# Reordering and merging the transfers behind a staged activation in a four-direction state-space kernel

## The chip, the cores and the metric

The kernel runs on one core of a Trainium2 chip. The metric is the device time of one execution in microseconds. The kernel before was timed in 3 runs: median 1778.31 us, from 1777.98 to 1785.43.

## What is computed

The input `x` is (4, 128, 96, 96) in float32. It is group-normalised (32 groups), read as a sequence of 9216 positions in four directions (rows forward and backward, columns forward and backward), sent through the same small network in each, and the four results are fused and added to `x`:

```python
t = grouped1x1(x, in_proj_w, in_proj_b)          # 4 groups, 128 -> 512 channels
u, gate = silu(t[:, :256]), t[:, 256:]
u = depthwise_conv(u, dw_w)                      # 5 taps along the sequence
s, bb, cc = ssm_in(u), tanh(ssm_b(u)), tanh(ssm_c(u))
a = 0.999 + 0.0009 * sigmoid(ssm_delta(u))
prefix = cumsum(log(a))
hst = exp(prefix) * cumsum(bb * s * exp(-prefix))  # h = a*h + bb*s
u = u + ssm_out(cc * hst + ssm_d * s)
y = out_proj(grouped1x1(u * sigmoid(gate), mix_w, mix_b))
out = x + fuse_w @ concat(y of the 4 directions) + fuse_b
```

All arithmetic is float32.

## The kernel before

**Tiling.** There are 8 phases, one for each batch and each axis (V, then H; phase 0 is batch 0's V). A phase walks its sequence from both ends at once, in 6 steps of 1536 positions; a step is split by the position's residue modulo 4 into 4 residues of 384 columns. One **iteration** (`pair_on(t)`, 24 to a phase, 192 in all; the first six are `pair(t)`) does one residue for the forward and the backward direction. Steps 12 to 17 are phase 2, iteration 48 is its first.

**Fresh and mirrored steps.** The first 3 steps of a phase are fresh: `x` is projected and its silu computed, for both ends. In the last 3 the two directions have swapped places, so the silus and gates of the first 3 serve again: those of steps 3 and 4 are still in SBUF, step 5's were written to DRAM during step 0 (`keep_silu`) and come back by `load_silu`; gates are all written to DRAM (`kept`) and read back by `load_kept`, 768 KB each, two iterations ahead.

**The front.** An iteration t prepares residue g of a step five iterations ahead (the *front* `ahead = t + 5`; a step's four fronts end two iterations before its first iteration). `new_front` gives four matmuls from `x_in` (two tiles, one for each end, four residues each); `new_silu` writes the second half of the channels straight into the step's `sil` tile; `new_stage` (L506-533) writes the first half into a staging tile (`shared` in the profile, L517), because the conv wants it with channels and residues exchanged, and four DMAs of 96 KB carry it over to `sil` (L525, `sil<-shared`). Behind them `new_stage` issues three loads of the next step's `x_in` (L297: 64, 32 and 32 partitions, since the last group of channels of the backward end uses residue g where the others use 3-g), and in step 0 the stores of the second half (L559, `sil<-sil`) and of the stage (L561, `front<-shared`); in other steps an `edge` store (L533). In step 0 the first column is zeroed by GpSimd (L521, L523) before those DMAs.

**Order.** The program is written out by hand, each engine runs its instructions in that order, and nearly all DMAs are issued by SyncE (SP). An iteration's DMAs stand in this order: loads of `lone`, reload of `acc` and store of `out` (L1050, L902: at the start of an H-to-V phase the finished batch leaves and the next comes in), statistics chunks `xs` of the next batch (L429, read by VectorE's `bn_stats` L437), gate loads, `load_kept` (L675), and the front's DMAs. Each of SP's DMAs signals one of eight semaphores, DMAHW0 to DMAHW7, in turn, and waits until the last DMA on the same one has landed: the ninth waits for the first, whatever its data. For example the chunk that iteration 51 reads:

```order
L429 DMA xs_3_5002<-in_xr 128x384 [waits DMAHW1_49,DVE_49]
```

Iteration t on TensorE is: `conv` (L130, `sil,band`, into banks 6 and 7, which the last stage must have left), the last pair's output products (`u,w_fin`), the front's matmuls (L490) between those of the state output (L638), and the projection (`u,main`), whose tanh on ScalarE is `tm` (L845). The first `conv` of a step needs all four quarters of `sil`. For residues 1 and 2 `conv_less` adds 16 short matmuls (`sil,less`).

**The opening.** Steps 0 and 1 are built from smaller projections (`compute_front`, `front_parts`); `whole_front` does a whole front of step 2 in each of `pair(4)` and `pair(5)`, and a second one at the end of `pair(5)`.

Of the kernel before, what the change touches and what calls it, by code (L numbers as in the profile page):

```python
# [68 lines left out]
def conv_preact_kernel(  # L69
# [55 lines left out]
    def bank(i):  # L125
        return psum[:, i, :]
# [160 lines left out]
    def half(s):  # L287
        return slice(64 * s, 64 * s + 64)
# [5 lines left out]
    def load_front(step, s, r, q):  # L294
        if fresh(step):
            un = units[step * UB + s]
            nc.sync.dma_start(  # L297
                x_in[s][r, q, :], xs[un["b"], un["lay"], r, q, bass.ds(un["st"] * N, N + 1)]
            )
# [146 lines left out]
    def sil_tile(of):  # L446
        return wk.tile([P, 2, 4, 2, N + 1], F32, tag="sil", name=f"sil_{of}")

    kept_sil = [dp.tile([R, P, 2, N + 1], F32, tag=f"sil{e}", name=f"sil{e}") for e in range(2)]
# [6 lines left out]
    def front_parts(i, banks, half=False):  # L456

        step, g = divmod(i, R)
        if g == 0:
            sils[step] = new_sil(step)  # L460
        yield from compute_front(step, g, banks, half)
        if g == R - 1:
            keep_lone(step)
        after_front(step, g)

    def mirrored(i):

        step, g = divmod(i, R)
        if step * UB >= NU or fresh(step):
            return  # L470
        st = step % NS
        if st in (NS // 2, NS // 2 + 1):
            sils[step] = sils[step - 1 - 2 * (st - NS // 2)]
        elif g < 3:
            load_silu(step, (g + 1,))
        if st == NS - 2:
            for s in range(2):
                load_front(step + 2, s, half(s), slice(g, g + 1))

    def new_front(i, banks):  # L480

        step, g = divmod(i, R)
        if g == 0:
            sils[step] = new_sil(step)
        st, r = step % NS, (0, 32, 64, 96)

        def one(s, j):
            q = R - 1 - g if s > j else g
            a = slice(64 * s + 32 * j, 64 * s + 32 * j + 32)
            nc.tensor.matmul(  # L490
                bank(banks[2 * j + s])[:, : N + 1], stats[units[step * UB]["b"]][0][a, s, :], x_in[s][a, q, :],
                start=True, stop=True,
            )

        return one

    def new_silu(i, banks):

        step, g = divmod(i, R)
        bn = stats[units[step * UB]["b"]][1]  # L500
        for s in range(2):
            nc.scalar.activation(  # L502
                sils[step][:, s, 1, g, :], bank(banks[2 + s])[:, : N + 1], AF.Silu, bias=bn[:, 1:2]
            )

    stages = []  # L506
# [1 line left out]
    def new_stage(i, banks):  # L508

        step, g = divmod(i, R)  # L510
        st, bn, sil = step % NS, stats[units[step * UB]["b"]][1], sils[step]
        if g == 0 and (st == 0 or step == 2):
            sh = shared()
            stages[:] = [sh[:, e * 2 * (N + 1) : (e + 1) * 2 * (N + 1)].rearrange("p (s n) -> p s n", s=2)
                         for e in range(2)]
        stage = stages[g % 2]
        nc.scalar.activation(  # L517
            stage, psum[:, banks[0] : banks[0] + 2, : N + 1], AF.Silu, bias=bn[:, 0:1]
        )
        if st == 0:  # L520
            nc.gpsimd.memset(stage[:, g // 2, 0:1], 0.0)  # L521
            if g < 2:
                nc.gpsimd.memset(sil[:, :, 1, g, 0:1], 0.0)  # L523
        for m in range(4):
            nc.sync.dma_start(sil[32 * g : 32 * g + 32, :, 0, m, :], stage[32 * m : 32 * m + 32, :, :])  # L525
        if st < NS // 2 - 1:
            load_front(step + 1, 0, slice(0, 64), slice(g, g + 1))
            load_front(step + 1, 1, slice(64, 96), slice(R - 1 - g, R - g))
            load_front(step + 1, 1, slice(96, P), slice(g, g + 1))
        if st == 0:  # L530
            keep_silu(step, g)
        elif g in (0, R - 1):
            nc.sync.dma_start(edge_of(step)[g // 3], stage)  # L533

    def whole_front(i, banks):
        one = new_front(i, banks)
        for s, j in ((0, 1), (0, 0), (1, 0), (1, 1)):
            one(s, j)
        new_silu(i, banks)
        new_stage(i, banks)  # L540

    def edges(step, g, j, engine):
        sil = sils[step]
# [13 lines left out]
    def keep_silu(step, g):  # L557
        e = step // NS % 2
        nc.sync.dma_start(kept_sil[e][g], sils[step][:, :, 1, g, :])  # L559
        if step:  # L560
            nc.sync.dma_start(kept_front[e][g], stages[g % 2])  # L561
        else:
            nc.sync.dma_start(by_group(kept_front[e], g), sils[step][32 * g : 32 * g + 32, :, 0].rearrange("c s m n -> c m s n"))

    def by_group(t, g):
        return t[g].rearrange("(m c) s n -> c m s n", m=4)

    def load_silu(step, gs):
        if 0 in gs:
            sils[step] = new_sil(step)  # L570
        for g in gs:
            e = step // NS % 2
            nc.sync.dma_start(sils[step][:, :, 1, g, :], kept_sil[e][g])
            nc.sync.dma_start(sils[step][32 * g : 32 * g + 32, :, 0].rearrange("c s m n -> c m s n"), by_group(kept_front[e], g))

    def in_proj(step, g, s, j, bk):
        for c in range(4):
# [84 lines left out]
    def keep(n):  # L662
        return kept[n // NP % 2][n % NP]
# [313 lines left out]
    def pair(t):  # L977
        i = 2 * t
        banks = head_banks(t)
        if t == R:  # L980
            load_lone(1)
        if t:
            new_u(i)
            taps(i, range(1, K))
            single = alone(units[i]["p"])
            conv(i, banks, single)
            if single:
                add_lone(i, banks)
# [23 lines left out]
        for g in {0: (0, 1), 1: (2, 3)}.get(t, ()):  # L1012
            keep_silu(0, g)
        if t > 3:
            nc.sync.dma_start(keep(t - 4), tile_of(t - 4))
        if t > 0:
            s = tbs[i - 2][0:64, :]
            nc.gpsimd.tensor_scalar(s, s, d_sb[0:64, 0:1], None, ALU.mult)

    def pair_on(t):  # L1020
# [106 lines left out]
        if gated is not None:  # L1127
            if gated % NP > 1:
                nc.sync.dma_start(keep(gated), to)
            else:  # L1130
                nc.sync.dma_start(keep(gated)[:, :, 0], both)
        load_kept(n + 2)
        if ahead is not None:
            new_stage(ahead, spots)
        if last:
            for s in range(2):
                under(bi + 2, s)
# [8 lines left out]
        if t >= end - 4:  # L1146
            load_last(t)
        if step % NS == NS - 2 and g == R - 1:
            load_silu(step + 1, (0,))
        if n % (NP * 2) == 0:  # L1150
            send()

# [288 lines left out]
```

## Time and profile before

| what | us |
|---|---|
| median of 3 runs | 1778.31 |
| the profiled execution | 1789.02 |
| its span, first to last instruction | 1787.2 |
| TensorE matmuls busy | 1724.5 (96%) |
| VectorE, ScalarE, GpSimd busy | 1515.0, 1478.2, 1459.8 |
| DMA queue of SP | 383.06 MB, 71.0% of the 16 engines' time |

A row of the timeline gives the start, the time from the first start to the last end, engine, line, operation, tiles written and read, shape, the count of instructions merged, and in brackets the idle time of the engine just before, with what ended it. TensorE's ends are modelled, so its busy share says little; its idle times in brackets say where the program stood still. For SP a row's length is the issuing alone. PEclk is the share of the clock that TensorE was granted.

### The profile page before, as it was taken

What the parts mean: (1) busy time and instruction counts of PE and PEld (TensorE: products, weight loads), DVE (VectorE), ACT (ScalarE), POOL (GpSimd) and SP (SyncE); (2) the same over time, 40 slices, a digit from 0 to 9 for tenths busy, and PEclk for the clock granted to TensorE, in tenths of its full rate; (3) what the DMA queues carried; (4) which work ended last, traced back from release to release, by engine and by line L of the source; (5) the groups of instructions that cost most, each with busy time, mean ns of one, the idle gap of its engine ahead of it and who ended that gap; (6) DMA issues with size and microseconds to landing.
All of it is one profiled execution on the core that took longest, in us unless ns stands there. A gap on an engine that the chain in (4) does not pass through costs nothing.

```text
span 1787.2 us, 50638 instructions
## 1 busy us (share of the span) xinstructions
PE 1724.5 (96%) x20410; PEld 707.6 (40%) x20410; DVE 1515.0 (85%) x1508; ACT 1478.2 (83%) x2410; POOL 1459.8 (82%) x1466
## 2 busy tenths in 40 slices
PE   7999999999889999999989999999998999999998
PEld 3243344344343334434434343344343443344333
DVE  5799989888688998888868998888876888888897
ACT  4788888888778888888878888888887888888875
POOL 3489988988669988988867998888876899888887
PEclk9999999999999999999999999999999999999999
DMA  7755996369895798537999489843899738973375
GB/s 215 224 169 181 298 247 177 138 212 262 248 280 207 225 272 226 169 122 248 251 257 315 149 258 265 230 136 131 263 263 272 227 130 271 235 205 126 129 236 177
DMA packets 156232, 386.33 MB, mean 216 GB/s; under 512 B 22624, under 2 KB 89056, under 8 KB 156000
## 3 DMA queue, kind: packets, MB, share of 16 engines
q1 hardware_dynamic: 155856, 383.06, 71.0%
q8 instruction: 162, 2.65, 0.6%
q14 instruction: 70, 0.57, 0.1%
q10 hardware_dynamic: 144, 0.04, 0.0%
HBM read 215.12 MB, written 133.01 MB: 195 GB/s over the span
## 4 chain that ended last, share of the span: by engine, by line
PE 81%; DMA 10%; ACT 2%; DVE 2%; POOL 2%; issue 1%; SPq 1%; ACTq 0%; DVEq 0%; POOLq 0%
PE psum L130 66%; PE psum L638 6%; PE psum L618 5%; PE psum L490 4%; DMA gate<-kept 4%; DMA x_in<-in_xs 2%; DMA sil<-shared 2%; DMA kept<-shared 1%; DVE psum L808 1%; DMA front<-shared 1%; DVE u L699 1%; POOL acc L943 1%; ACT shared L517 1%; ACT psum L806 1%; DMA sil<-sil 1%
## 5 line engine op out<-in xcount | busy, mean ns | idle before, releaser
L808 DVE SCALAR_TENSOR_TENSOR psum<-sil,small,psum 128x768 f32<-128x768 f32 x576 | 589.1, 1023 | 51.9 <-ACT psum L806 33.3
L130 PE MATMUL psum<-u,w_fin 128*32 128x384 f32 (+1 forms) x6192 | 559.2, 486 | 1.1 <-ACT ys L924 0.5
L130 PE MATMUL psum<-u,main 128*32 128x384 f32 x6144 | 536.1, 490 | 0.6 <-DVE u L755 0.4
L699 DVE SCALAR_TENSOR_TENSOR u<-gate,psum 128x768 f32<-128x768 f32 x376 | 341.6, 950 | 156.9 <-PE psum L638 73.3
L943 POOL TENSOR_TENSOR acc<-ys,acc 128x384 f32<-128x384 f32 x375 | 433.8, 1178 | 19.6 <-ACT ys L924 7.3
L130 PE MATMUL psum<-sil,band 128*32 128x384 f32 x3072 | 300.3, 497 | 40.8 <-DMA sil<-shared 12.9
L130 PEld LDWEIGHTS psum<-u,w_fin 128*32 128x32 f32 x6192 | 204.9, 110 | 312.0 <-issue 212.1
L889 POOL TENSOR_TENSOR t<-t,t 64x384 f32<-64x384 f32 (+1 forms) x192 | 268.9, 1400 | 68.6 <-DVE t L883 36.0
L650 ACT COPY psum<-u 128x768 f32<-128x768 f32 x384 | 306.3, 798 | 7.2 <-DVE u L699 4.4
L130 PEld LDWEIGHTS psum<-u,main 128*32 128x32 f32 x6144 | 180.2, 110 | 327.1 <-issue 206.9
L856 POOL TENSOR_SCALAR t<-tm 64x384 f32<-64x384 f32 x188 | 177.6, 945 | 142.1 <-ACT tm L845 123.2
L638 PE MATMUL psum<-t,main 32*128 32x384 f32 x1536 | 273.1, 519 | 3.0 <-ACT psum L650 2.3
L890 POOL TENSOR_TENSOR t<-t,t 64x384 f32<-64x384 f32 (+1 forms) x192 | 235.0, 1224 | 15.1
L857 POOL TENSOR_TENSOR t<-t,tm 64x384 f32<-64x384 f32 x192 | 220.0, 1146 | 25.1 <-ACT t L848 10.0
L808 DVE SCALAR_TENSOR_TENSOR u<-sil,small,psum 128x768 f32<-128x768 f32 x192 | 194.9, 1015 | 6.8
L806 ACT ACTIVATE psum<-sil,small 128x768 f32<-128x768 f32 x191 | 171.7, 899 | 32.9 <-DVE u L699 31.5
L926 ACT COPY ys<-psum 128x384 f32<-128x384 f32 x288 | 137.9, 479 | 60.0 <-PE psum L130 51.0
L130 PEld LDWEIGHTS psum<-sil,band 128*32 128x32 f32 x3072 | 108.4, 110 | 197.2 <-issue 82.5
L618 PE MATMUL psum<-x_in,wn 32*128 32x384 f32 x768 | 162.2, 497 | 0.0
L490 PE MATMUL psum<-x_in,wn 32*128 32x385 f32 x704 | 150.1, 503 | 1.5 <-DMA x_in<-in_xs 1.4
L502 ACT ACTIVATE sil<-psum,bnorm 128x385 f32<-128x385 f32 x176 | 102.3, 582 | 54.8 <-PE psum L490 39.4
L654 ACT ACTIVATE gate<-psum,bnorm 128x384 f32<-128x384 f32 x168 | 97.2, 581 | 43.8 <-PE psum L618 27.0
(110 smaller groups left out, 1708.5 us busy)
## 6 DMA issues: line engine op xcount, KB each, us to landing
gate<-kept SPq DMA_DIRECT2D x106, 768.0 KB, 7.4
kept<-gate SPq DMA_DIRECT2D x82, 768.0 KB, 3.9
sil<-shared SPq DMA_DIRECT2D x352, 96.2 KB, 5.9
x_in<-in_xs SPq DMA_DIRECT2D x306, 96.2 KB, 3.8
sil<-sil SPq DMA_DIRECT2D x64, 385.0 KB, 5.9
lone<-edge SPq DMA_DIRECT2D x26, 770.0 KB, 8.5
out<-acc SPq DMA_DIRECT2D x46, 384.0 KB, 5.6
acc<-in_xr SPq DMA_DIRECT2D x39, 384.0 KB, 5.2
```

Of the source, the lines that this page charges most:

```text
L130: nc.tensor.matmul(o[r, : rhs.shape[-1]], lhsT, rhs, start=start, stop=stop, skip_group_check=True)
L490: nc.tensor.matmul(bank(banks[2 * j + s])[:, : N + 1], stats[units[step * UB]["b"]][0][a, s, :], x_in[s][a, q, :], start=True, stop=True,)
L618: nc.tensor.matmul(bank(to)[:, :N], stats[un["b"]][0][r, s, :], x_in[s][r, q, off : off + N], start=True, stop=True)
L638: nc.tensor.matmul(bank(ssm(bi, s) + j)[:, :N], w_so[r, bass.ts(j, P)], z[r, :], start=(bi, s) not in seeded, stop=True, skip_group_check= ...
L650: nc.scalar.copy(psum[:, ssm(bi, s) : ssm(bi, s) + 2, :N], us[bi][:, s])
L699: nc.vector.scalar_tensor_tensor(v, g, 1.0, pz, ALU.add, ALU.mult)
L806: nc.scalar.activation(part, src, AF.Copy, scale=w_tap[:, 0:1])
L808: nc.vector.scalar_tensor_tensor(us[i][:, :, 1, :] if k == K - 1 else part, src, w_tap[:, k : k + 1], part, ALU.mult, ALU.add,)
L857: nc.gpsimd.tensor_mul(ta[0:64, p, :], tb[0:64, :], tm[0:64, :])
L889: engine.tensor_mul(ta[0:64, p, r], tb[64:P, r], ta[64:P, p, r])
L890: engine.tensor_add(tb[0:64, r], ta[0:64, p, r], tb[0:64, r])
L943: adder.tensor_add(part, y, part)
```

## The change

1. In `pair_on`, `new_stage` with its four `sil<-shared` DMAs now comes ahead of `load_kept`; what followed those DMAs is split off into `new_rest`, behind `load_kept`.
2. The backward end's last group uses residue 3-g like the others, so `x_in` is loaded two residues at a time (`load_planes`), one DMA for each end, after every second front: 4 DMAs for a step in place of 12. The first step of the next phase is loaded in iterations 9 and 10 of a phase (4 DMAs) where it was 8 DMAs in iterations 12 to 15.
3. The second half of step 0's silus is stored and reloaded two residues at a time (770 KB in place of 385), and the store moves from step 0's four fronts to the first two fronts of step 1 (iterations 23 and 0 of the phase).
4. The stage's zero column is written by ScalarE right behind the stage; GpSimd's remaining memset is one for each front.
5. In the opening the second front of `pair(5)` moves into `pair_on(6)`, between its `conv` and its output products, in banks 4 and 5 used twice; `after_front`'s loads of `x_in` come ahead of `keep_lone`'s four stores.

SP's DMAs fall from 1405 to 1233 (`x_in` 436 to 296, step 0's stores and reloads 64 to 32); ScalarE gets 28 instructions more; TensorE's and VectorE's counts stay. The core of the diff:

```diff
-        load_kept(n + 2)
         if ahead is not None:
             new_stage(ahead, spots)
+        load_kept(n + 2)
+        if ahead is not None:
+            new_rest(ahead)
+        if t % NP in (9, 10) and un["step"] // NS < 2 * B - 1:
+            load_planes((un["step"] // NS + 1) * NS, t % NP - 9)
...
+    def load_planes(step, h):
+        for s in range(2):
+            load_front(step, s, half(s), bass.ts(1 - h if s else h, 2))
...
         def one(s, j):
-            q = R - 1 - g if s > j else g
+            q = R - 1 - g if s else g
...
         if st == 0:
-            nc.gpsimd.memset(stage[:, g // 2, 0:1], 0.0)
-            if g < 2:
-                nc.gpsimd.memset(sil[:, :, 1, g, 0:1], 0.0)
+            nc.scalar.activation(stage[:, g // 2, 0:1], mid, AF.Copy, scale=0.0)
+            nc.gpsimd.memset(sil[:, g // 2, 1, min(g, R - 1 - g), 0:1], 0.0)
         for m in range(4):
             nc.sync.dma_start(sil[32 * g : 32 * g + 32, :, 0, m, :], stage[32 * m : 32 * m + 32, :, :])
-        if st < NS // 2 - 1:
-            load_front(step + 1, 0, slice(0, 64), slice(g, g + 1))
-            load_front(step + 1, 1, slice(64, 96), slice(R - 1 - g, R - g))
-            load_front(step + 1, 1, slice(96, P), slice(g, g + 1))
+
+    def new_rest(i):
+        step, g = divmod(i, R)
+        st, stage = step % NS, stages[g % 2]
+        if st < NS // 2 - 1 and g % 2:
+            load_planes(step + 1, g // 2)
         if st == 0:
-            keep_silu(step, g)
+            nc.sync.dma_start(kept_front[step // NS % 2][g], stage)
         elif g in (0, R - 1):
             nc.sync.dma_start(edge_of(step)[g // 3], stage)
+        if st == 1 and step > 1 and g < 2:
+            keep_silu(step - 1, g)
...
-        if t == LAG - 1:
-            whole_front(t + R + 1, (6, 7, 2, 3))
...
+        if n == 0:
+            i0, to = t + R, (4, 5, 4, 5)
+            one = new_front(i0, to)
+            one(0, 1)
+            one(1, 1)
+            new_silu(i0, to)
+            one(0, 0)
+            one(1, 0)
+            new_stage(i0, to)
+            new_rest(i0)
         add_next(w[0])
```

How the order of instructions changes, at three places. First SP in iterations 45 and 46, where the last two quarters of step 12 are staged (`sil_4335` and `sil_4305` are step 12's tile before and after, `gate` the tiles of the kept gates). Before:

```order
L675 DMA gate_177<-kept_4_194 128x1536
L525 DMA sil_4335<-shared 32x770 x4
L297 DMA x_in_70<-in_xs 64x385
L297 DMA x_in_71<-in_xs 32x385 x2
L559 DMA sil_202<-sil_4335 128x770
L561 DMA front_204<-shared 128x770
L675 DMA gate_176<-kept_7_197 128x1536
L525 DMA sil_4335<-shared 32x770 x4
L297 DMA x_in_70<-in_xs 64x385
L297 DMA x_in_71<-in_xs 32x385 x2
L559 DMA sil_202<-sil_4335 128x770
L561 DMA front_204<-shared 128x770
```

The same two iterations after:

```order
L525 DMA sil_4305<-shared 32x770 x4
L686 DMA gate_177<-kept_4_194 128x1536
L534 DMA front_204<-shared 128x770
L525 DMA sil_4305<-shared 32x770 x4
L686 DMA gate_176<-kept_7_197 128x1536
L297 DMA x_in_70<-in_xs 64x2x385
L297 DMA x_in_71<-in_xs 64x2x385
L534 DMA front_204<-shared 128x770
```

The quarter's four DMAs stand ahead of the gate's, and 20 DMAs have become 14.

Second SP in iterations 49 to 51, with the statistics chunk `xs_3` that VectorE reads in iteration 51 and the last quarter of step 13 (`sil_4730`, `sil_4690`), of iteration 50. Before:

```order
L1050 DMA acc<-in_xr 128x2x384 x2
L902 DMA out<-acc 128x2x384 x2
L675 DMA gate_177<-kept_0_190 128x1536
L525 DMA sil_4730<-shared 32x770 x4
L297 DMA x_in_70<-in_xs 64x385
L297 DMA x_in_71<-in_xs 32x385 x2
L429 DMA xs_3_5002<-in_xr 128x384
L675 DMA gate_176<-kept_3_193 128x1536
L525 DMA sil_4730<-shared 32x770 x4
```

After, from the end of iteration 48 on:

```order
L297 DMA x_in_70<-in_xs 64x2x385
L297 DMA x_in_71<-in_xs 64x2x385
L565 DMA sil_202<-sil_4305 128x1540
L1059 DMA acc<-in_xr 128x2x384 x2
L913 DMA out<-acc 128x2x384 x2
L525 DMA sil_4690<-shared 32x770 x4
L686 DMA gate_177<-kept_0_190 128x1536
L429 DMA xs_3_4957<-in_xr 128x384
L525 DMA sil_4690<-shared 32x770 x4
```

The three loads of `x_in` just ahead of the chunk are gone; farther ahead the doubled store of the silus (`sil_202`, 770 KB) and the doubled `x_in` loads of iteration 48 have come in.

Third TensorE in the opening, from the end of `pair(5)`'s projection (`u_1_2_0`) to the first state outputs (L638, L649). Before:

```order
L130 MATMUL psum<-u_1_2_0_788,main 32x384 x16
L490 MATMUL psum<-x_in_70,wn_265 128x385 x2
L490 MATMUL psum<-x_in_71,wn_265 128x385 x2
L130 MATMUL psum<-sil_443,band 32x384 x8
L490 MATMUL psum<-x_in_70,wn_265 128x385
L638 MATMUL psum<-t_0_0_1_0_442,main 128x384 x3
```

After:

```order
L130 MATMUL psum<-u_1_2_0_786,main 32x384 x16
L130 MATMUL psum<-sil_443,band 32x384 x8
L491 MATMUL psum<-x_in_70,wn_265 128x385
L491 MATMUL psum<-x_in_71,wn_265 128x385
L491 MATMUL psum<-x_in_70,wn_265 128x385
L491 MATMUL psum<-x_in_71,wn_265 128x385
L491 MATMUL psum<-x_in_70,wn_265 128x385
L649 MATMUL psum<-t_0_0_1_0_442,main 128x384 x3
```

The four matmuls of the second front now follow the `conv` and no longer precede it; their second two use the banks of the first two.

More of the change, by code (lines that the diff above doesn't have):

```diff
@@ L447, in sil_tile @@
         return wk.tile([P, 2, 4, 2, N + 1], F32, tag="sil", name=f"sil_{of}")
-    kept_sil = [dp.tile([R, P, 2, N + 1], F32, tag=f"sil{e}", name=f"sil{e}") for e in range(2)]
+    kept_sil = [dp.tile([2, P, 2, 2, N + 1], F32, tag=f"sil{e}", name=f"sil{e}") for e in range(2)]
     kept_front = [dp.tile([R, P, 2, N + 1], F32, tag=f"front{e}", name=f"front{e}") for e in range(2)]
@@ L461, in front_parts @@
         yield from compute_front(step, g, banks, half)
+        after_front(step, g)
         if g == R - 1:
             keep_lone(step)
-        after_front(step, g)
     def mirrored(i):
@@ L474, in mirrored @@
         elif g < 3:
[L475 to L478, printed above, removed]
+            load_silu(step, g + 1)
+    def load_planes(step, h):
+        for s in range(2):
+            load_front(step, s, half(s), bass.ts(1 - h if s else h, 2))
     def new_front(i, banks):
@@ L502, in new_silu @@
             nc.scalar.activation(
-                sils[step][:, s, 1, g, :], bank(banks[2 + s])[:, : N + 1], AF.Silu, bias=bn[:, 1:2]
+                sils[step][:, s, 1, R - 1 - g if s else g, :], bank(banks[2 + s])[:, : N + 1], AF.Silu, bias=bn[:, 1:2]
             )
@@ L540, in whole_front @@
         new_stage(i, banks)
+        new_rest(i)
     def edges(step, g, j, engine):
@@ L1011, in pair @@
             load_gate(2 * n + s + UB)
-        for g in {0: (0, 1), 1: (2, 3)}.get(t, ()):
-            keep_silu(0, g)
+        if t < 2:
+            keep_silu(0, t)
         if t > 3:
@@ L1148, in pair_on @@
         if step % NS == NS - 2 and g == R - 1:
-            load_silu(step + 1, (0,))
+            load_silu(step + 1, 0)
         if n % (NP * 2) == 0:
```

29 lines of the change are left out of this document (16 added, 13 removed).

## The prediction

> **What bounds the kernel now.** I read the page first, then TensorE's idle times in its timeline, then who was late at each of them. The page's rows:
>
> ```profile
> span 1787.2 us, 50638 instructions
> ...
> PE 1724.5 (96%) x20410; PEld 707.6 (40%) x20410; DVE 1515.0 (85%) x1508; ACT 1478.2 (83%) x2410; POOL 1459.8 (82%) x1466
> ...
> sil<-shared SPq DMA_DIRECT2D x352, 96.2 KB, 5.9
> ```
>
> TensorE sets the pace; nothing in the change takes a matmul away. What can be won is the time in which it stands still. TensorE's timeline, the waits over 1 us behind the start-up's first, with the `conv`s of two undisturbed iterations (473.39 and 481.75) for comparison:
>
> ```profile
> 66.37 2.30 PE L490 MATMUL psum<-x_in,wn 32*128 32x385 f32 x6 [1.41 <-DMA x_in<-in_xs]
> ...
> 81.16 2.79 PE L130 MATMUL psum<-sil,band 128*32 128x384 f32 x16 [2.20 <-ACT shared L517]
> ...
> 238.61 1.67 PE L130 MATMUL psum<-sil,band 128*32 128x384 f32 x14 [1.22 <-DMA sil<-shared]
> ...
> 453.31 3.14 PE L130 MATMUL psum<-sil,band 128*32 128x384 f32 x16 [4.06 <-DMA x_in<-in_xs]
> ...
> 473.39 1.48 PE L130 MATMUL psum<-sil,band 128*32 128x384 f32 x16
> ...
> 481.75 1.48 PE L130 MATMUL psum<-sil,band 128*32 128x384 f32 x16
> ...
> 497.16 3.26 PE L130 MATMUL psum<-sil,band 128*32 128x384 f32 x14 [6.86 <-DMA sil<-shared]
> ...
> 640.66 1.50 PE L130 MATMUL psum<-sil,band 128*32 128x384 f32 x16 [1.15 <-ACT shared L517]
> ...
> 677.05 2.02 PE L130 MATMUL psum<-sil,band 128*32 128x384 f32 x14 [1.19 <-ACT shared L517]
> ...
> 890.26 1.70 PE L130 MATMUL psum<-sil,band 128*32 128x384 f32 x15 [2.15 <-DMA x_in<-in_xs]
> ...
> 934.37 3.06 PE L130 MATMUL psum<-sil,band 128*32 128x384 f32 x14 [8.15 <-ACT t L854]
> ...
> 1113.26 2.08 PE L130 MATMUL psum<-sil,band 128*32 128x384 f32 x14 [1.17 <-ACT shared L517]
> ...
> 1327.21 3.22 PE L130 MATMUL psum<-sil,band 128*32 128x384 f32 x16 [2.81 <-DMA x_in<-in_xs]
> ...
> 1368.99 3.18 PE L130 MATMUL psum<-sil,band 128*32 128x384 f32 x14 [4.77 <-DMA sil<-shared]
> ...
> 1549.62 2.13 PE L130 MATMUL psum<-sil,band 128*32 128x384 f32 x15 [2.55 <-ACT t L854]
> ```
>
> They add up to 39.7 us, and but for the first two they lie at the seams of phases. I sort them: **A**, first `conv` of phases 2, 4, 6 (453, 890, 1327): 9.02. **B**, first of phases 1, 3, 5, 7 (238, 677, 1113, 1549): 6.13. **C**, first `conv` of the second step of phases 2, 4, 6 (497, 934, 1369): 19.78. D, at 640.66: 1.15. The opening: 3.61. A `conv` after a wait also runs slower than the 1.48 us of 481.75: 1.66, 0.22 and 1.74 more in A (3.62), 1.98 in B, 5.06 in C. So A costs 12.6 us, B 8.1, C 24.8.
>
> Why A: ScalarE's timeline has the stage of step 12's last quarter (iteration 46), SP's timeline when it was sent; the last two rows are from SP's waits and from the DMA issues between 440.7 and 492.1 us (count, size, median us to landing).
>
> ```profile
> 439.59 0.89 ACT L517 ACTIVATE shared<-psum,bnorm 128x770 f32<-128x770 f32 x1
> ...
> 441.37 0.35 SPq L559 DMA_DIRECT2D sil<-sil  x1
> ...
> 443.13 0.38 SPq L675 DMA_DIRECT2D gate<-kept  x1
> 443.85 2.45 SPq L525 DMA_DIRECT2D sil<-shared  x4
> ...
> 452.92 0.34 SPq L559 DMA_DIRECT2D sil<-sil  x1
> ...
> SPq L559 <- DMA gate<-kept: 37.7, 22, 4.1
> ...
> sil<-shared SPq DMA_DIRECT2D x19, 96.2 KB, 7.5
> ```
>
> The stage ends at 440.48. SP is then still busy with iteration 45's stores: a store of this line waits for the landing of a gate, with which it shares nothing but a semaphore, 22 times for 37.7 us in all. The four transfers leave 3.4 us late, behind 768 KB of gate, and the `conv` that could start at 449.25 (453.31 less 4.06) starts at 453.31.
>
> Why C: the same lag, grown to an iteration. VectorE's rows (statistics, and the gating that frees the gate's tile), then SP's:
>
> ```profile
> 470.21 1.82 DVE L699 SCALAR_TENSOR_TENSOR u<-gate,psum 128x768 f32<-128x768 f32 x2 [1.07 <-ACT ys L924]
> ...
> 485.78 0.55 DVE L437 BATCH_NORM_STATS2 bn<-xs 128x6 f32<-128x384 f32 x1
> 492.15 0.56 DVE L437 BATCH_NORM_STATS2 bn<-xs 128x6 f32<-128x384 f32 x1 [5.81 <-DMA xs<-in_xr]
> ...
> 673.79 0.56 DVE L437 BATCH_NORM_STATS2 bn<-xs 128x6 f32<-128x384 f32 x1 [1.80 <-DMA xs<-in_xr]
> ...
> 479.91 0.47 SPq L675 DMA_DIRECT2D gate<-kept  x1
> ...
> 484.16 1.97 SPq L297 DMA_DIRECT2D x_in<-in_xs  x3
> 489.79 0.35 SPq L429 DMA_DIRECT2D xs<-in_xr  x1
> ```
>
> The gate whose tile was free at 472.03 is asked for at 479.91. The chunk, eight DMAs behind that gate, waits for its landing: SP issues nothing from 486.13 to 489.79. VectorE then stands 5.81 us, and the quarter behind the chunk keeps TensorE 6.86 us. The row at 673.79 shows the same, smaller, behind B's two waits on ScalarE.
>
> **The change part by part, against the profiled 1789.02 us.**
>
> *Staged silus first, fewer DMAs: A.* In step 0's iterations SP now has 6 or 8 DMAs where it had 10. Eight places ahead of iteration 46's first quarter transfer stands a store of iteration 45, landed by then, so it leaves at 440.5. Four issues at 0.61 (2.45 over 4) and the page's median landing of 5.9 us give 448.8, under 449.25. With the 7.5 us of the crowded stretch, taken behind the gates, it would be 1.2 us late. Nearest is the page's median, since the gate now stands behind: A goes, -12.6 (bounds -12.6, since no more is there, and -7 with 1.2 us left at each and one restart).
>
> Here a rule of the Trainium skill can be weighed. The waits of 2.15 and 2.81 us were followed by a `conv` of 1.70 and of 3.22 us, so I count 1.74 us of slow restart with the second. The Trainium skill, "TensorE: Matmul & The Clock Gate", Part 1, has the clock halved only after an idle window of about 3.4 us; by it the 1.74 would have another cause and A would give 10.9. The trace's row decides: it counts.
>
> *B.* The same cause: at 238 the quarter itself is late, at 677 the chunk (673.79 in VectorE's rows), behind which gating and stage stand. With fewer DMAs ahead of both, of 8.1 I take 7, as for A all but a remainder (bounds 4 and 8.1).
>
> *C.* Here bytes count too. What moved between iteration 46's stage and the chunk's landing, and the rate of that stretch beside that of the densest 20 us (columns of the last two: stretch, length, busy time of each engine, PEclk, DMA share, GB/s):
>
> ```profile
> q1 hardware_dynamic: 6054, 12.64, 86.6%
> ...
> sil<-sil SPq DMA_DIRECT2D x2, 385.0 KB, 4.9
> ...
> 440.70:492.10 51.40, 45.53 (x516) 20.03 (x508) 34.82 (x36) 36.94 (x60) 34.49 (x35) 0.97 0.87 248
> 500.00:520.00 20.00, 20.00 (x241) 8.22 (x237) 14.00 (x14) 15.86 (x26) 13.90 (x14) 0.98 1.04 304
> ```
>
> After, two stores of 385 KB and a front's of the same size leave the stretch and two of 770 KB come in: +0.39 MB, 13.0 MB. At 248 GB/s that takes 52.4 us, at 304 42.8. The chunk is wanted when VectorE has done the one before it, 486.33 (485.78 and 0.55), less the 5.7 us that A's first wait and restart no longer cost: 39.9 us after 440.70. So it is late by 2.9 to 12.5 us, where it is late by 5.81. The quarter (0.39 MB more) is wanted when the projection is through, 490.30 less 5.7, 43.9 us after: late by 0.2 to 10.1, now 6.86. The middles are about today's waits, so C stays at phases 2 and 4. At phase 6 no statistics are loaded (four chunks, 0.79 MB less): the quarter is late by -2.5 to +6.9 against 4.77; I take half of its 6.5 (wait and restart) away: -3. Bounds for all of C: -24.8 and +16.
>
> *Zero column.* No activation of one column lies in a front today; the nearest row is at the start:
>
> ```profile
> 2.53 0.20 ACT L341 ACTIVATE first_table<-first_table 128x1 f32<-128x1 f32 x1
> ```
>
> 28 of them: 5.6 us if all stood on the path, below nothing if GpSimd's memset had held a transfer. The stage's transfers wait for it, TensorE does not: I take +1.
>
> *Opening.* SP's rows, the stores and then the loads that end the first wait:
>
> ```profile
> 59.00 3.43 SPq L739 DMA_DIRECT2D edge<-sil  x4
> 62.53 2.47 SPq L297 DMA_DIRECT2D x_in<-in_xs  x4
> ```
>
> The loads now leave 3.5 us sooner: -1.4. The 2.20 us at 81.16 (the second front's stage holds bank 6) go, but that front now stands behind the `conv` and must wait for its own silus between its two pairs of matmuls: 0 (bounds -2.2 and +2). `x_in` two residues at a time arrives after every second front, three iterations before use; D keeps its cause: both nothing.
>
> Sum: -12.6 - 7 - 3 + 1 - 1.4 = -23.0. The profiled execution is 10.7 us above the median. The waits with their restarts are 50.4 us of it; if the 10.7 lie wholly in them, the gain shrinks to 0.79 of that, -18.1. From 1778.31 that gives 1755.3 to 1760.2; I take 1757.
>
> **The rivals.**
>
> *C goes as well.* For it: fewer DMAs mean fewer empty stretches of SP like 486.13 to 489.79, and 13.0 MB in 39.9 us is 326 GB/s, little over the 304 that was seen for 20 us. Against it: nothing here held 326 for 40 us. Price: another 21.8, with the 0.79 at least 17: 1735 to 1740. The Trainium skill, "DMA: Bandwidth & Descriptors", Specifications, puts the limit of a core's HBM traffic at about 358 GB/s; by that this rival would hold, the trace's 304 speaks against it.
>
> *C grows.* The doubled stores now lie where C is tightest. If the rate stays at 248, the chunks of phases 2 and 4 come 6.7 us later than today, the three quarters about 3: +13 to +16 over my sum, 1770 to 1773.
>
> *Gates come late: slower.* `load_kept` now waits for ScalarE's stage and four issues, some 3.5 us more. A gate has two iterations, about 17.4 us (two of the 8.36 between the `conv`s at 473.39 and 481.75, and some). Today the one of 479.91 was asked for 7.9 us late and landed just before the chunk's issue, 9.8 us on: 17.7, hidden because VectorE stood still anyway. If SP's lag stays over 4 us, gatings of iterations 49 to 51 wait some 4 us each: three seams, three gatings, +36: 1793. For it: nothing but order has changed for the gate. Against: the lag is what the fewer DMAs take away.
>
> *No effect.* The quarter lands late for lack of rate, not of order: 1778.
>
> **How the numbers follow.** Forecast 0.54 (alone 1748 to 1767), C gone 0.18, C grown 0.17, gates late 0.06, no effect 0.05. The bounds of A and B move each case by some 6 us, so the range 1735 to 1775 leaves out half of C gone, a third of C grown and the late gates, 0.2 in all. Beyond 0.5%, about what a measurement of this kernel can tell from no change (1769.4 and 1787.2): faster 0.76 (forecast, C gone, a quarter of C grown), same 0.19, slower 0.05.
>
> **What would show it.** Right: the waits at the first `conv` of phases 1 to 7 under 0.5 us with `conv`s of 1.5 us, SP's `sil<-shared` leaving within 0.5 us of the stage; `bn_stats` of iteration 51 still waiting about 6 us and the next `conv` about 7. Wrong: A's waits still 2 us or more; C under 3 us in all three places; VectorE's gating waiting for `gate<-kept`; the chain through ScalarE longer in iterations 19 to 22.

## The result and the profile after

The changed kernel takes 1760.85 us (median of 4 runs, 1758.79 to 1763.52) against 1781.57 of the kernel before in the same comparison; the ratio is 0.9884, 95% interval 0.9853 to 0.9915. The profiled execution took 1758.79 us, 30.2 less than that of before, which was a long one of its kind. The forecast of 1757 us, with its range of 1735 to 1775, holds; one term of its sum has the wrong sign, as will be seen.

The page after:

```profile
span 1757.0 us, 50266 instructions
...
PE 1713.8 (98%) x20410; PEld 705.5 (40%) x20410; DVE 1508.5 (86%) x1508; ACT 1484.5 (84%) x2438; POOL 1470.6 (84%) x1452
...
gate<-kept SPq DMA_DIRECT2D x106, 768.0 KB, 5.7
...
sil<-shared SPq DMA_DIRECT2D x352, 96.2 KB, 3.5
```

A quarter now lands 3.5 us after its issue (median), where it was 5.9. TensorE's timeline: first `conv`s of phases 2 and 4, then all waits over 1 us behind the opening.

```profile
442.59 1.75 PE L130 MATMUL psum<-sil,band 128*32 128x384 f32 x16
...
472.38 1.57 PE L130 MATMUL psum<-sil,band 128*32 128x384 f32 x16 [2.62 <-ACT shared L518]
...
485.33 1.68 PE L130 MATMUL psum<-sil,band 128*32 128x384 f32 x15 [2.85 <-ACT shared L518]
...
872.21 1.62 PE L130 MATMUL psum<-sil,band 128*32 128x384 f32 x16
...
901.82 1.50 PE L130 MATMUL psum<-sil,band 128*32 128x384 f32 x16 [2.57 <-ACT shared L518]
...
914.89 3.19 PE L130 MATMUL psum<-sil,band 128*32 128x384 f32 x16 [4.45 <-ACT shared L518]
...
1342.91 2.06 PE L130 MATMUL psum<-sil,band 128*32 128x384 f32 x15 [2.74 <-ACT shared L518]
```

The rows without brackets had no wait: A and B are gone. C is still there, but in two pieces in phases 2 and 4, and it is ScalarE's stage that is late, not the quarter itself. ScalarE is late because VectorE was; its waits for DMAs in these stretches:

```profile
469.62 1.82 DVE L710 SCALAR_TENSOR_TENSOR u<-gate,psum 128x768 f32<-128x768 f32 x2 [3.44 <-DMA gate<-kept]
...
482.11 0.56 DVE L437 BATCH_NORM_STATS2 bn<-xs 128x6 f32<-128x384 f32 x1 [4.97 <-DMA xs<-in_xr]
...
899.05 1.82 DVE L710 SCALAR_TENSOR_TENSOR u<-gate,psum 128x768 f32<-128x768 f32 x2 [3.40 <-DMA gate<-kept]
...
911.67 0.56 DVE L437 BATCH_NORM_STATS2 bn<-xs 128x6 f32<-128x384 f32 x1 [5.10 <-DMA xs<-in_xr]
...
1340.15 1.82 DVE L710 SCALAR_TENSOR_TENSOR u<-gate,psum 128x768 f32<-128x768 f32 x2 [4.42 <-DMA gate<-kept]
```

So each C now begins with a late gate, which is the mechanism of the rival "gates come late", once in a seam and not three times, and in phases 2 and 4 goes on with a late chunk. VectorE's gating waiting for a kept gate was one of the prediction's own signs of being wrong.

**Where the time went.** For all kernels below I measure one thing: the length of an iteration, from the start of its `tm` on ScalarE to that of the next. ScalarE's timeline for iterations 48 to 51 after:

```profile
451.61 0.58 ACT L856 ACTIVATE tm<-psum,small 128x384 f32<-128x384 f32 x1
...
460.81 0.58 ACT L856 ACTIVATE tm<-psum,small 128x384 f32<-128x384 f32 x1
...
472.24 0.57 ACT L856 ACTIVATE tm<-psum,small 128x384 f32<-128x384 f32 x1
...
485.18 0.57 ACT L856 ACTIVATE tm<-psum,small 128x384 f32<-128x384 f32 x1
...
494.40 0.58 ACT L856 ACTIVATE tm<-psum,small 128x384 f32<-128x384 f32 x1
```

They last 9.20, 11.43, 12.94 and 9.22 us. As undisturbed I take 9.20, 8.42, 8.25 and 9.22 (in experiment 11, where nobody waits there, phase 6 has 9.20, 8.42, 8.36 and 9.26), so C costs 7.7 us here. The same sum over iterations 0 to 5 of phases 2, 4 and 6 I call C, that over iterations 20 to 23 of the seven seams AB (undisturbed 8.88, 8.33, 8.26, 9.31 at the end of a V phase, 9.20, 8.43, 8.33, 9.23 of an H phase; with the zero column by ScalarE iteration 22 takes 8.01, which makes the small negative sums). Slow restarts and waits inside a `conv` are in both. The medians come from four comparisons, in which the kernel before took 1780.27 to 1784.28 us; the sums are of one profiled execution each.

| kernel | timed median, us | profiled execution, us | AB | C | sum |
|---|---|---|---|---|---|
| before | 1781.57 | 1789.02 | 22.5 | 28.3 | 50.8 |
| changed | 1760.85 | 1758.79 | -1.2 | 23.2 | 22.0 |
| changed, timed again | 1757.07 | 1759.06 | -1.5 | 22.0 | 20.5 |
| order only | 1763.44 | 1764.09 | 12.1 | 16.1 | 28.2 |
| x_in in pairs only | 1763.37 | 1766.45 | 8.5 | 24.8 | 33.3 |
| changed, gate ahead | 1758.42 | 1758.97 | -1.4 | 21.1 | 19.7 |
| changed, zeros by GpSimd | 1763.76 | 1761.79 | 0.2 | 25.0 | 25.2 |
| zeros by GpSimd, old opening | 1766.01 (one run) | 1766.01 | 0.4 | 27.0 | 27.4 |
| changed, stores early | 1753.45 | 1756.78 | -1.1 | 22.1 | 21.0 |
| changed, chunks moved | 1753.45 | 1754.14 | -1.2 | 17.7 | 16.5 |
| chunks moved, gate ahead | 1751.37 | 1751.32 | -1.5 | 14.9 | 13.4 |
| chunks moved, stores early | 1747.72 | 1750.55 | -1.4 | 13.6 | 12.2 |
| no stores (work left out) | 1744.10 | 1744.22 | -1.2 | 9.3 | 8.1 |
| no stores, chunks moved | 1736.08 | 1734.82 | -1.1 | 0.5 | -0.6 |

From before to after the two sums fall by 28.8 us. The first `tm` also comes 3.1 us earlier (41.5 and 38.4 us from the start; 36.9 to 41.5 over all the runs, ahead of anything that the change touches), the first seven iterations take 2.6 less (55.2 and 52.6), and iterations 17 to 19 of the seven phases 3.8 more (3.3 and 7.1 over undisturbed). Together that is 30.7 us, for the 30.2 between the two executions.

What replaced the waits is seen in the stretch from 450 to 500 us. Its columns are length, busy time of PE, PEld, DVE, ACT, POOL, PEclk, DMA share, GB/s. Before:

```profile
450.00:500.00 50.00, 39.83 (x432) 18.60 (x436) 34.70 (x36) 33.35 (x54) 32.73 (x33) 0.91 0.87 250
```

After:

```profile
450.00:500.00 50.00, 44.53 (x512) 17.96 (x508) 38.12 (x38) 38.01 (x62) 34.28 (x34) 0.97 1.03 296
```

Before, the 16 DMA engines were idle for an eighth of this stretch, since SP stood at its semaphores. After, they are full (a full set reads a little over 1 in this view). C was a question of SP's order and of bytes; experiments 4 to 7 and 11 ask how far it is now one of bytes.

### The profile page after: what moved, and what is told of

Read it like the earlier page. It is cut to its first block, busy times and chain, and to the rows that moved or that the text cites. A ratio compares the mean times of both kernels' runs of the same rounds, so it can differ in the third digit from the quotient of the medians.

```text
span 1757.0 us, 50266 instructions
## 1 busy us (share of the span) xinstructions
PE 1713.8 (98%) x20410; PEld 705.5 (40%) x20410; DVE 1508.5 (86%) x1508; ACT 1484.5 (84%) x2438; POOL 1470.6 (84%) x1452
## 4 chain that ended last, share of the span: by engine, by line
PE 86%; DMA 5%; DVE 2%; ACT 2%; POOL 2%; issue 1%; SPq 0%; ACTq 0%; POOLq 0%; DVEq 0%
PE psum L130 70%; PE psum L649 6%; PE psum L629 5%; PE psum L491 4%; DMA gate<-kept 2%; DMA kept<-shared 1%; DMA out<-acc 1%; ACT shared L518 1%; DVE t L894 1%; DMA sil<-shared 1%; DVE u L710 1%; DVE psum L819 1%; DMA acc<-in_xr 1%; POOL t L900 0%; POOL t L868 0%
## 5 line engine op out<-in xcount | busy, mean ns | idle before, releaser
L954 POOL TENSOR_TENSOR acc<-ys,acc 128x384 f32<-128x384 f32 x375 | 442.0, 1202 | 12.5 <-ACT ys L935 1.9
L130 PE MATMUL psum<-sil,band 128*32 128x384 f32 x3072 | 290.1, 489 | 19.6 <-ACT shared L518 18.0
L649 PE MATMUL psum<-t,main 32*128 32x384 f32 x1536 | 272.8, 520 | 3.0 <-ACT psum L661 2.3
L868 POOL TENSOR_TENSOR t<-t,tm 64x384 f32<-64x384 f32 x192 | 227.0, 1182 | 25.4 <-ACT t L859 10.3
L937 ACT COPY ys<-psum 128x384 f32<-128x384 f32 x288 | 138.4, 481 | 53.1 <-PE psum L130 42.6
```

Source lines behind the costliest of these rows:

```text
L130: nc.tensor.matmul(o[r, : rhs.shape[-1]], lhsT, rhs, start=start, stop=stop, skip_group_check=True)
L649: nc.tensor.matmul(bank(ssm(bi, s) + j)[:, :N], w_so[r, bass.ts(j, P)], z[r, :], start=(bi, s) not in seeded, stop=True, skip_group_check= ...
L868: nc.gpsimd.tensor_mul(ta[0:64, p, :], tb[0:64, :], tm[0:64, :])
L954: adder.tensor_add(part, y, part)
```

## The experiments

**1. Part 1 alone.** The kernel before, with the stage's four transfers ahead of the gate (what follows them is split off as `new_rest`, as in the change; the cut shows the calls alone):

```diff
-        load_kept(n + 2)
         if ahead is not None:
             new_stage(ahead, spots)
+        load_kept(n + 2)
+        if ahead is not None:
+            new_rest(ahead)
```

> The kernel before with part 1 alone: the four transfers of a stage ahead of the kept gate, everything else (twelve loads of x_in a step, stores in step 0, GpSimd's zeros, the opening) as before. Theory 'order': in step 0 the first two quarter transfers no longer stand behind a gate, so A's waits (9.0 us and 3.6 us of slow restart) fall under 1 us each and B halves; C stays at 20 us or more: 1762 to 1768. Rival 'count': the lag of SP comes from ten DMAs in an iteration, and the third and fourth quarter transfers still wait for the landing of the gate eight places ahead; A loses less than a third and the time is 1773 to 1780.

1763.44 us, ratio 0.9869 (0.984 to 0.9899). The time is what "order" said, but the split is not: AB only halves (12.1), and C falls to 16.1, at phase 6 to 0.4. At the three seams of A 3.3 us are left of 13.2, at the four of B 8.9 of 9.3. Of the waits at first `conv`s these stand in TensorE's timeline (phases 1, 2 and 3; phase 5 has one more, of 2.12 us, and within phase 0 one of 3.01 us has come in):

```profile
236.37 1.72 PE L130 MATMUL psum<-sil,band 128*32 128x384 f32 x16 [1.26 <-ACT shared L517]
...
448.31 2.15 PE L130 MATMUL psum<-sil,band 128*32 128x384 f32 x15 [1.61 <-ACT shared L517]
...
668.80 2.67 PE L130 MATMUL psum<-sil,band 128*32 128x384 f32 x16 [2.50 <-DMA gate<-kept]
```

So the order by itself takes most of A and hardly any of B. Why C shrinks beside it stays open. It is not that time lost at AB lets the queue catch up: the seam ahead of phase 6, where C all but goes (8.3 to 0.4), lost 0.6 us here and 4.6 before.

**2. Part 1 alone undone.** The changed kernel with the gate ahead again:

```diff
+        load_kept(n + 2)
         if ahead is not None:
             new_stage(ahead, spots)
-        load_kept(n + 2)
-        if ahead is not None:
             new_rest(ahead)
```

> The changed kernel with part 1 alone undone: the kept gate ahead of the stage's four transfers again. Theory 'order': A and B come back in part, 1 to 2 us with a slow restart at each of seven seams: 1766 to 1774; gating's three waits for gate<-kept (11.3 us in the changed kernel) go. Rival 'count': after parts 2 and 3 SP has no lag left at A and B, where the last quarter lands 4 us ahead of its use, so putting 768 KB of gate (2.6 us at the 297 GB/s of the crowded stretch) in front hides; A and B stay under 0.5 us, and since the gate comes earlier C shrinks: 1752 to 1760.

1758.42 us, ratio 0.9845 (0.982 to 0.9869), no slower than the changed kernel. AB is gone as before (-1.4), C is 21.1. "Count" holds. VectorE's waits:

```profile
DVE bn L437 <- DMA xs<-in_xr: 9.1, 3, 5.3
...
DVE u L710 <- DMA gate<-kept: 3.9, 1, 3.9
```

The gate's waits fall from 11.3 us to 3.9, but quarters take their place: TensorE waits 5.58 and 5.41 us in phases 4 and 6.

```profile
912.17 3.19 PE L130 MATMUL psum<-sil,band 128*32 128x384 f32 x15 [5.58 <-DMA sil<-shared]
...
1343.22 3.23 PE L130 MATMUL psum<-sil,band 128*32 128x384 f32 x14 [5.41 <-DMA sil<-shared]
```

In this full queue the order chose who waited, and hardly how long.

**3. x_in in pairs alone.** The kernel before, six loads in a step in place of twelve, the gate ahead of the stage as it was:

```diff
-        if st < NS // 2 - 1:
-            load_front(step + 1, 0, slice(0, 64), slice(g, g + 1))
-            load_front(step + 1, 1, slice(64, 96), slice(R - 1 - g, R - g))
-            load_front(step + 1, 1, slice(96, P), slice(g, g + 1))
+        if st < NS // 2 - 1 and g % 2:
+            h = g // 2
+            load_front(step + 1, 0, slice(0, 64), bass.ts(h, 2))
+            load_front(step + 1, 1, slice(64, 96), bass.ts(1 - h, 2))
+            load_front(step + 1, 1, slice(96, P), bass.ts(h, 2))
```

> The kernel before with its x_in loads two residues at a time after every second front, three DMAs for each (six a step in place of twelve); the rest, the gate ahead of the stage among it, as before. Theory 'either will do': SP's lag goes with fewer DMAs as it goes with the order, so A and B lose half or more: 1762 to 1770, iterations 22 and 23 of the even seams under 10 us each. Rival 'order': the quarters still stand behind a gate, A and B stay: 1775 to 1783.

1763.37 us, ratio 0.99 (0.9883 to 0.9916): "either will do". No first `conv` of a phase waits over 1 us, though iteration 23 still takes 10.6 to 11.1 us at five seams, more than the 10 that I expected at the even ones. C stays at 24.8. Of A 5.1 us are left, of B 3.4. So the order alone and the count alone each bring most of the change's gain; their gains overlap at A, while B falls with the count and not with the order. In the changed kernel the order could be taken back without loss.

**4. Statistics chunks a phase later.** The changed kernel, with the four chunks that phases 2 and 4 read in iterations 2 and 3 read in the next phase, as phase 0 does:

```diff
-        places = singles * 2
-        if ph == 0:
-            places = (singles[2:] + [NP + 2, NP + 3]) * 2
+        places = (singles[2:] + [(ph + 1) * NP + 2, (ph + 1) * NP + 3]) * 2
```

> The changed kernel with the four statistics chunks that phases 2 and 4 read in their iterations 2 and 3 read in iterations 2 and 3 of phases 3 and 5 (phase 0 does so already). Theory 'bytes': the waits of C come from 0.79 MB more than the queue carries there at 297 GB/s; without the chunks phases 2 and 4 lose in their iterations 1 to 3 what phase 6, which has none, loses (5.1 us over undisturbed iterations in place of 7.9 and 10.7): 8 us less, 1750 to 1754, bn_stats waits under 1 us. Rival 'gate': the late gate alone sets C, the chunk's wait only lies beside it: within 2 us of the changed kernel, 1758 to 1762.

1753.45 us, ratio 0.982 (0.9794 to 0.9846), the time that "bytes" said, though C falls by some 5 us where it said 8. What is left of C is all gate; the waits for chunks lie elsewhere:

```profile
DVE u L708 <- DMA gate<-kept: 17.7, 4, 5.9
...
DVE bn L435 <- DMA xs<-in_xr: 1.8, 3, 1.1
```

Phase 2 gained little (7.2 us of C, 7.7 with the chunks), phase 4 most (5.4, 10.5).

**5. Stores of kept silus left out.**

```diff
-        if st == 1 and step > 1 and g < 2:
+        if st == 1 and 1 < step < 2 * NS and g < 2:
```

> The changed kernel without the two stores of kept silus (770 KB each) in phases 2 to 7; the reloads read what phases 0 and 1 stored, so step 5's second half of silus is another batch's. Theory 'bytes': 1.54 MB less at 297 GB/s is 5.2 us of queue ahead of the late gate and chunk at each seam, so of the 23.7 us that C costs now 10 to 15 go: 1745 to 1751. Rival 'gate': the stores stand behind the gate that is late and the lateness is SP's waits for semaphores, so less than 4 us go: 1757 to 1761.

1744.10 us, ratio 0.9765 (0.9741 to 0.9789). C falls from 23.2 to 9.3, a fall within the 10 to 15 us expected, and is 0.1 at phase 6.

**6. The same stores in step 0 again.**

```diff
-        if st == 1 and step > 1 and g < 2:
-            keep_silu(step - 1, g)
+        if st == 0 and g % 2:
+            for s in range(2):
+                h = s if g == 1 else 1 - s
+                nc.sync.dma_start(kept_sil[step // NS % 2][h][:, :, s, :], planes_of(step, h)[:, :, s, :])
```

> The changed kernel with the kept silus stored in step 0 again, two residues of one end at a time: two stores of 385 KB after the second front and two after the fourth (iterations 20 and 22 of a phase) in place of two of 770 KB in iterations 23 and 0. Theory 'bytes': C comes from what the saturated queue carries between iterations 23 and 2; 1.54 MB less there leaves what the kernel without these stores had, about 9 us of C and none at phase 6, and 770 KB more (2.6 us at 297 GB/s) in iterations 20 and 22 hide, since the last quarters there land 4 us ahead of their use: 1745 to 1751. Rival 'A back': stores in the fronts make the quarters late again, as in the kernel with part 1 alone, whose iterations 22 and 23 lost 11.5 us: 1754 to 1762.

1753.45 us, ratio 0.9851 (0.9835 to 0.9867). Both theories miss: AB stays away (-1.1), and C hardly moves (22.1). The time is lower than the changed kernel's by less than the two intervals tell apart. The stores fill a gap between 430 and 440 us, where the DMA share goes from 0.68 to 0.92, and still nothing is won. Stretches after:

```profile
430.00:440.00 10.00, 10.00 (x115) 4.56 (x115) 7.32 (x8) 8.73 (x15) 9.39 (x11) 1.00 0.68 217
...
460.00:470.00 10.00, 9.76 (x116) 3.92 (x108) 6.32 (x8) 6.79 (x12) 9.23 (x10) 1.00 1.04 258
```

With the stores early:

```profile
430.00:440.00 10.00, 10.00 (x116) 4.49 (x118) 7.53 (x8) 8.57 (x16) 9.39 (x11) 1.00 0.92 265
...
460.00:470.00 10.00, 8.62 (x100) 3.47 (x96) 8.33 (x10) 7.47 (x12) 8.62 (x10) 1.00 1.06 234
```

From 460 to 470 the full engines move only 234 GB/s. Why a stretch with fewer bytes to carry is slower stays open. Bytes alone do not set C, then: experiment 1 too stores in step 0, with other loads of `x_in` and other zeros, and its C at phase 6 is 0.4 us, where this kernel's is 5.1.

**7. Both.** Edits 4 and 6 together:

> The two together: stores in step 0, and the statistics chunks of iterations 2 and 3 of phases 2 and 4 read one phase later. Theory 'bytes': phases 2 and 4 then carry what phase 6 does, so C is under 1 us in all three: 1736 to 1743. Rival: C has a part that hangs on neither, 1745 or more.

1747.72 us, ratio 0.9819 (0.9805 to 0.9834): the rival's side. C keeps 13.6 us, all of it gating's wait for gates (19.7 us, 6 times). Against edit 4 alone the ratio is the same.

**8. Zeros by GpSimd and the old opening.** Two edits that lie apart, in one run:

```diff
-            nc.scalar.activation(stage[:, g // 2, 0:1], mid, AF.Copy, scale=0.0)
+            nc.gpsimd.memset(stage[:, g // 2, 0:1], 0.0)
...
+        if t == LAG - 1:
+            whole_front(t + R + 1, (6, 7, 2, 3))
...
-        if n == 0:
-            i0, to = t + R, (4, 5, 4, 5)
...
```

> The changed kernel with two edits undone that lie apart in the profile: GpSimd's memset for the stage's zero column, and the opening as it was (second front in iteration 5, edge stores ahead of x_in). From the kernels that ran, the zero column on ScalarE costs 0.26 us in iteration 19 of an even seam and nothing in the others (about 1 us in all), and the first seven iterations take 33.6 us with either opening: iteration 19 at 9.4 us in place of 9.6, the first seven within 1 us of 33.7, the time within 3 us of the changed kernel. Rival (the prediction's sum): the opening costs 1.4 us more, and ScalarE's column 0.2 in each of 28 fronts, 5.6 us less.

1766.01 us in the one run, 5.2 more than the changed kernel, where I expected 3 at most. The first seven iterations take 52.9 us (52.6 in the changed kernel), and 52.6 and 53.1 in experiments 1 and 3, which have the old opening too; the kernels with the new one spread from 52.6 to 53.9. (The 33.6 and 33.7 of the expectation are iterations 3 to 6 alone.) So the opening's part is worth nothing that shows, and the 55.2 of the profile before was that execution's own. Iteration 19 is 9.37 to 9.40 us long, as expected, where it is 9.62. But C is 27.0, and that asked for the next run.

**9. Zeros by GpSimd alone**, timed beside the changed kernel on one chip:

> The changed kernel once more, beside the other three on one chip: 1757 to 1763. The theories expect the same.

> The changed kernel with part 4's new operation alone undone: GpSimd's memset writes the stage's zero column. Theory 'GpSimd holds the transfers': the stage's four DMAs wait for GpSimd, which comes to its memset 4.5 us after the stage (126.5 us in 28 fronts in the run with zero column and opening undone); SP stands still with all that is behind, and C and the kept gates of iterations 17 and 18 cost 3 to 7 us more: 1762 to 1768. Rival 'nothing either way' (the prediction took +1 for ScalarE's column): within 2 us of the changed kernel, the 1766 of that run being its scatter.

The first edit of 8 alone. 1757.07 us (1755.8 to 1760.4) for the changed kernel and 1763.76 (1761.79 to 1769.62) with GpSimd's memset; no two runs overlap. The zero column by ScalarE is worth 6.7 us. ScalarE's stage, GpSimd's memset and SP's transfers of one front, first with GpSimd's zero:

```profile
418.35 0.89 ACT L518 ACTIVATE shared<-psum,bnorm 128x770 f32<-128x770 f32 x1
...
421.51 0.10 POOL L522 MEMSET shared<- 128x1 f32 x1
...
421.64 3.13 SPq L525 DMA_DIRECT2D sil<-shared  x4
```

The same front of the changed kernel, timed again:

```profile
418.32 0.89 ACT L518 ACTIVATE shared<-psum,bnorm 128x770 f32<-128x770 f32 x1
419.24 0.20 ACT L522 ACTIVATE shared<-mid 128x1 f32<-128x1 f32 x1
...
419.47 2.42 SPq L525 DMA_DIRECT2D sil<-shared  x4
```

The memset takes 0.1 us, but GpSimd comes to it 2.3 us after the stage, and SP stands for it with the gate and all else behind. With GpSimd's zero the lengths of two iterations of phase 1 grow by 3.7 us together, AB by 1.7 and C by 3.0, and iterations 17 to 19 shrink by 3.3. In SP's waits the row for this is 124.6 us in 28 fronts here. In the kernel before it stands too, smaller since SP came late itself; GpSimd reaches its memset as late there (up to 2.7 us after the stage, here up to 2.8):

```profile
SPq L525 <- POOL sil L523: 29.8, 14, 3.2
```

**10. Chunks moved, gate ahead.** Edits 2 and 4 together:

> The changed kernel with part 1 undone (gate ahead of the stage's transfers) and the statistics chunks moved a phase on. With the chunks moved all that is left of C are gating's waits for the gate (17.7 us). Theory 'order': the gate ahead of 394 KB and four issues lands 2 to 3 us sooner, three to five times: C at 8 to 10, 1743 to 1748. Theory 'bytes': the quarter then waits in the gate's place, as with the gate ahead and the chunks in place (C 21.1 against 23.2); at most 2 us less than with the chunks moved alone: 1750 to 1755.

1751.37 us (1745.73 to 1755.14), ratio 0.9823 (0.9793 to 0.9854): on the side of "bytes". The gate's waits go from 17.7 us to 4.0, C from 17.7 to 14.9, and most of it lies in phase 6 now (8.9).

**11. Both kinds of bytes away.** Edits 4 and 5 together:

> Chunks moved, and the stores of kept silus left out in phases 2 to 7 (step 5's second half of silus is another batch's). Theory 'bytes': without the chunks phases 2 and 4 are what phase 6 was without stores, where C was 0.1 us; so C under 1 us in all three, 9 us less than without the stores alone: 1734 to 1739. Rival: the two overlap, C keeps 3 us or more: 1739 to 1745.

1736.08 us, ratio 0.9738 (0.9704 to 0.9773). C is 0.5 us. Behind the opening TensorE has no wait over 1 us in any iteration, and VectorE waits for chunks 1.5 us in all and for no gate. The same stretch as above:

```profile
450.00:500.00 50.00, 50.00 (x597) 20.55 (x590) 42.74 (x42) 44.83 (x73) 41.06 (x42) 1.00 1.02 295
```

The engines are as full as after the change (1.02, 295 GB/s); there is just enough less to carry. This shows what C hangs on: 2.36 MB a seam at phases 2 and 4 (two stores of 770 KB, four chunks of 192). The stores had to be left out for it; moved two to three iterations ahead, as in experiment 7, they leave 13.6 us of C.

**A better version.** The three kernels that compute all of the reference with the chunks moved (4, 7 and 10) lie at 0.9819 to 0.9823 of the kernel before, against 0.9857 (0.9826 to 0.9889) and 0.9884 of the changed one. Number 7 has the narrowest interval, 0.9805 to 0.9834, and the lowest median, 1747.72 us; the intervals do not tell the three apart.

## Why the prediction was right, step by step

**A, -12.6, and B, -7: right, a little small.** AB fell from 22.5 to -1.2 us, by 13.7 at A's seams and 10.1 at B's, the second past the bound of 8.1. The quarter of iteration 46 leaves at once, as the text asked (ScalarE's timeline after, then SP's):

```profile
433.09 0.90 ACT L518 ACTIVATE shared<-psum,bnorm 128x770 f32<-128x770 f32 x1
434.02 0.20 ACT L522 ACTIVATE shared<-mid 128x1 f32<-128x1 f32 x1
```

```profile
434.25 2.43 SPq L525 DMA_DIRECT2D sil<-shared  x4
436.78 0.53 SPq L686 DMA_DIRECT2D gate<-kept  x1
```

But the reason given for A, new order and fewer DMAs together, was one remedy more than needed: with the gate ahead AB is gone too, and the order alone takes most of A and hardly any of B.

**C stays, -3: right.** C lost 5.1 us. The rate went up to 296 GB/s over 450 to 500 us, near the 304 that the text took as its upper bound, and the seam is bound by it. VectorE still waits for the chunk 4.97 and 5.10 us (5.81 and 7.48 before). The next `conv` was to wait about 7 us still; it waits 2.85 and 4.45, and the `conv` before it 2.62 and 2.57. The half of phase 6's wait that was to go went (8.3 to 4.9). The rival "C goes as well" needed 326 GB/s for 40 us. The Trainium skill, "DMA: Bandwidth & Descriptors", Specifications, gives about 358 GB/s as a core's limit to HBM; the seam's mix of transfers, some of them within SBUF, does not reach it over these 50 us: with a DMA share of 1.03 it moves 296.

**Gates late: the mechanism came, its price did not.** The text put 12 us on each seam; gating waits 3.4 to 4.4 us once, and as experiment 2 shows, a chunk or a quarter would have waited there instead.

**Zero column, +1: wrong sign.** This step failed: "below nothing if GpSimd's memset had held a transfer" was named and then set aside, though SP's waits had the row. ScalarE's own price was fair: in iterations 17 to 23 the column costs 3.3 - 1.7 = 1.6 us. What it takes away, 6.7 us net, was the larger thing. With the lag of SP gone, GpSimd was the next to be late, and here the text did not ask what would be late next.

**Opening, -1.4: nothing that shows.** 52.9 us for the first seven iterations with the old one, 52.6 with the new.

**The sum.** -23.0 was foreseen between the profiled executions and 28.8 us went at the seams: A and B were larger than their waits and restarts as counted (22.5 us of lost time for 20.7), all of it went, and the hold by GpSimd, which the sum had not, was part of what lay in AB and C. The medians differ by 20.7 us, inside the 18.1 to 23.0 given for them. That it came so close is in part luck, since misses cancel: A, B and C fell by 28.8 us where 22.6 were foreseen; against that iterations 17 to 19 grew by 3.8, where 1 was put down for the column, and the opening's 1.4 did not show. The range did not hang on it: with the zeros left to GpSimd the time is 1763.76 us, inside it too.

## What to carry to other kernels

When a queue's issuer stands at semaphores while its consumers wait, ask first whether the DMA engines are full in that stretch: while their share was 0.87, order and count of the transfers won here, and either brought most of it; at 1.0 bytes left out of the stretch won, a new order mostly named another engine to wait, and bytes moved a little ahead in the same queue won next to nothing, for a reason that stays open. Price a tiny operation by when its engine gets to it, not by its length: 0.1 us of memset held four transfers for 2.3 us. Undo each part of a change singly, since here two parts held much of the same gain, and the one that was taken for a cost held another.

## What was not expected of the hardware

TensorE's clock halved here after a wait of little more than 2 us. In the kernel without stores, a `conv` after 2.27 us of idling takes 3.09 us, and the granted clock of the 2 us behind is 0.50:

```profile
480.82 3.09 PE L130 MATMUL psum<-sil,band 128*32 128x384 f32 x16 [2.27 <-ACT shared L518]
```

```profile
482.00:484.00 2.00, 2.00 (x16) 1.51 (x12) 1.93 (x3) 1.50 (x3) 1.92 (x3) 0.50 1.07 359
```

After the change a wait of 2.85 us (485.33 above) is followed by a `conv` of 1.68. The Trainium skill, "TensorE: Matmul & The Clock Gate", Part 1, asks for an idle window of about 3.4 us that runs free of the program; that the outcome varies with the moment agrees with the free-running window, that 2.27 us were enough does not agree with its length. The prediction's counting of the 1.74 us behind a wait of 2.81 was right: in the kernel before the granted clock is 0.50 from 1328 to 1330 us, just behind that wait.
